# Attention: pieces of other work in halves, between the two pairs of scores of a step

## The chip, the cores and the metric

The kernel runs on one core of one Trainium2 chip. The metric is the device time of one execution in microseconds (us). Before the change the median of three runs is 5130.76 us (5127.3 to 5130.8).

## The reference

A sequence of 4096 rows of width 256 goes through four stages, each added to its input: attention, expert layer, attention, expert layer.

```
x = x + attention_a(layernorm(x))
x = x + experts(layernorm(x))
x = x + attention_b(layernorm(x))
x = x + experts(layernorm(x))
```

Both attentions have 16 heads of width 16 and a causal mask. Attention a also adds exp(denom_bias) to each row's sum of exponentials and has a bias behind its output weights. Per head:

```
sim   = q @ k.T / 4, masked above the diagonal
e     = exp(sim - max(sim))
out   = (e @ v) / (sum(e) [+ exp(denom_bias)])
y     = concat(out over heads) @ Wo.T [+ bo]
```

The expert layer computes logits of 4096 rows against 2048 slots (64 experts of 32), two softmaxes of them (over slots and over experts), the slots' inputs, a small matrix product per expert, and the weighted sum back to the rows.

## The kernel before

All matrix work is float32. The rows stay in SBUF as `x`, 32 tiles of 128 rows. An attention takes the rows in 8 blocks of 512 and the heads in 4 groups of 4; a unit is one group in one block of queries, and the units run block after block, 32 in all. Keys and queries are split into a high and a low part (`split`, L165), so that two passes of reduced precision add up to float32; the parts are written to DRAM (`kd`, `qd`) and read back in the layout that the scores need (`load_to`, L345).

A unit needs two passes. Pass A (`steps_a`, L367) computes scores with queries on the partitions and takes each row's maximum on VectorE (L388 for blocks on the diagonal, with the mask added, L394 for the others). `finish_a` negates the maxima and sends them through DRAM into a layout in which a matmul can add them. Pass B (`steps_b`, L446) computes the scores transposed, keys on the partitions. One of its steps handles 128 keys: two pairs of heads, and for each pair two matmuls of keys and queries (`sc<-q,k`), two that subtract the maxima (`sc<-qm,one`), and one exponential on ScalarE (L471). On the diagonal GpSimd sets what lies above it to zero (L475), and the scores are narrower by `off` columns. `weigh` (V in what follows, L426) multiplies the exponentials of a step by the values, one step later. Every unit ends with `epilogue`: the sums go through DRAM to be inverted (`invert`), the output is divided on GpSimd (`divide`), and after four groups it is fetched again (`fetch`) and projected (`project`, L530).

TensorE's order is the program's. The loop at L601 writes it by hand: a step's two pairs of scores, half of the pass A work that is due (`wanted` spreads pass A of later units over the steps), a piece of other work (`net.beside`), V of the step before, the rest of pass A. Pass A, the pieces and the projections take their PSUM banks in turn from one pool of three (`net.bank`); the scores of pass B have two buffers of two banks, V one bank. Instructions of other engines are placed by the framework's scheduler, unless the code pins them.

`net.beside(n)` (L79) advances a clock by n, calls what is due (`invert`, `divide`, `fetch`), and then takes one piece, from `urgent` (projections) or from `side`. The side pieces of a block (`pieces`, L186) prepare the keys, queries and values of the block four ahead: four normalizations on GpSimd, two turns (four transposes each), four of keys and queries (512 columns each, `part`), two of values (`dense_values`), with empty places between. Blocks 0 and 1 of the second attention are prepared in the last loop of the first expert stage, one piece per tile from tile 7 on; what is left then runs after that loop, with one PSUM bank. Blocks 2 and 3 (and 0 and 1 of the first attention) are made all at once ahead of the steps, by `dense`.

Of the kernel before, what the change touches and what calls it, by code (L numbers as in the profile page):

```python
# [19 lines left out]
P = 128  # L20
S = 4096
D = 256
NT = S // P
QB = 512
NQB = S // QB
H = 16
HD = 16
# [15 lines left out]
class _Net:  # L43
# [22 lines left out]
    def mm(self, *a, **k):  # L66
        self.tc.keep_in_program_order(self.nc.tensor.matmul(*a, **k))  # L67
# [38 lines left out]
class _Attention:  # L106
# [55 lines left out]
            nc.gpsimd.tensor_tensor(x[:, t, :], x[:, t, :], self.bot, ALU.add)  # L162
        return y

    def split(self, ps, cc, dst, key, part=None):  # L165
        nc = self.net.nc
        two = part is not None
        if not two:
            part = self.hl[self.nhl % 2]
            self.nhl += 1  # L170
        hi, lo = part[:, 0, :], part[:, 1, :]
        nc.scalar.copy(hi.bitcast(F32R), ps)
        nc.vector.tensor_tensor(lo.bitcast(F32R), ps, hi, ALU.subtract)
        if key:
            nc.sync.dma_start(
                dst[ts(cc, 8)].bitcast(F32).rearrange("h e r l t -> (h e) r (l t)"),
                part.rearrange("p l t -> p (l t)").unsqueeze(1).to_broadcast([P, 2, 2 * QB]),
            )
            return
        for r in range(2):  # L180
            (nc.scalar if two and r else nc.sync).dma_start(
                dst[ts(cc, 8), :, :, r].bitcast(F32).rearrange("h e l t -> (h e) l t"), part
            )


    def pieces(self, b, fast=False, values=True):  # L186
        net, nc = self.net, self.net.nc
        xb, ys = self.xb[b % 2], {}
        idle = lambda: None

        def scale(i):
            if i == 0:
                self.begin(b)
            ys[i] = self.norm(4 * b + i, fast)

        def turn(t2):
            ps = net.bank().rearrange("p (c i t) -> p c i t", c=2, i=2)
            for i in range(2):
                for c in range(2):
                    net.tr(ps[:, c, i, :], ys[2 * t2 + i][:, ts(c, P)])  # L200
            nc.scalar.copy(xb[:, :, ts(t2, 2 * P)], ps.rearrange("p c i t -> p c (i t)"))

        def part(w, cc, key):
            ps = net.bank()
            for c in range(2):
                net.mm(ps, w[:, c, ts(cc, P)], xb[:, c, :], start=c == 0, stop=c == 1)
            self.split(ps, cc, (self.kd if key else self.qd)[b], key)

        out = []
        for t2 in range(2):  # L210
            out += [lambda i=i: scale(i) for i in (2 * t2, 2 * t2 + 1)]
            out += [idle, lambda t2=t2: turn(t2), idle]
        for w, key in ((self.wk, True), (self.wq, False)):
            out += [lambda a=(w, cc, key): part(*a) for cc in range(2)]
        if values:
            out += self.dense_values(b)
        return out

    def values(self, b, t2, ps):
        net, xb = self.net, self.xb[b % 2]  # L220
        ps = ps.rearrange("p (i d) -> p i d", i=2)
        for i in range(2):
            for c in range(2):
                net.mm(
                    ps[:, i, :], xb[:, c, ts(2 * t2 + i, P)], self.wv[:, c, :],
                    start=c == 0, stop=c == 1,
                )
        net.nc.scalar.copy(
            self.vah[:, ds(4 * b + 2 * t2, 2), :, 0:HD],
            ps.rearrange("p i (h e) -> p i h e", e=HD),  # L230
        )
# [32 lines left out]
    def run(self, ready, experts):  # L264

        net, tc, nc = self.net, self.net.tc, self.net.nc
        x, mm = net.x, net.mm
        bo, db = self.bo, self.db
        self.xd = net.xd = net.xds.pop(0)
        with ExitStack() as ctx:  # L270
            pool = lambda n, b, **k: ctx.enter_context(tc.tile_pool(name=f"at_{n}", bufs=b, **k))
            cp = pool("c", 1)
            wo = self.wo
# [10 lines left out]
                out=maskw, in_=maskw, compare_op=ALU.is_ge, fill=NEG,  # L284
# [11 lines left out]
            for p in range(2):  # L296
                f = net.ep.tile([P, QB], F32, name="ot", bufs=3)[:, 0:P]
                nc.gpsimd.memset(f, 0.0)
                for h2 in range(2):
                    for l in range(2):  # L300
                        nc.gpsimd.affine_select(
                            out=f, in_=f, compare_op=ALU.not_equal, fill=1.0,
# [30 lines left out]
            def third():  # L333
                actx.close()
                pairs.extend([psb, pool("psc", 1, space=PSUM)])
                net.banks = pool("psx", 1, space=PSUM)
# [148 lines left out]
            def epilogue(u, ot):  # L485
                g, b = units[u]
                if g == 0:
                    self.ad[b] = net.dram.tile([2 * P, QB], F32, name=f"{self.name}o{b}")
                d16 = net.ep.tile([P, 16], F32, name="d16", bufs=3)
                dd = net.dram.tile([P, 16], F32, name="dd", bufs=3)  # L490
                nc.sync.dma_start(d16, ot[HD:P:32, :].rearrange("j (c s) -> j c s", s=16))
                rb = {}

                def invert():
                    if db is not None:
                        nc.vector.tensor_scalar(d16, d16, edb[:, g : g + 1], None, ALU.add)
                    nc.vector.reciprocal(d16, d16)
                    rb[0] = net.ep.tile([P, QB], F32, name="rb")
                    nc.sync.dma_start(dd, d16)
                    nc.sync.dma_start(  # L500
                        rb[0],
                        dd.rearrange("(j c) s -> j (c s)", j=HG).unsqueeze(1)
                        .to_broadcast([HG, 32, QB]),
                    )
                    net.after(8, divide)

                def divide():
                    on = rb[0]
                    nc.gpsimd.tensor_tensor(on, ot, on, ALU.mult)
                    for j in range(HG):  # L510
                        nc.sync.dma_start(
                            self.ad[b][ds((HG * g + j) * HD, HD), :], on[ds(32 * j, HD), :]
                        )
                    if g == NG - 1:
                        net.after(4, fetch)

                back = {}

                def fetch():
                    for i2 in range(2):  # L520
                        ao = net.ep.tile([P, 2, 2 * P], F32, name="ao", bufs=2)
                        nc.sync.dma_start(
                            ao, self.ad[b].rearrange("(c p) t -> p c t", p=P)[:, :, ts(i2, 2 * P)]
                        )
                        back[i2] = ao
                    net.after(
                        8, lambda: net.urgent.extend([lambda: project(0), lambda: project(1)])
                    )

                def project(i2):  # L530
                    ps = net.bank().rearrange("p (i d) -> p i d", i=2)
                    for i in range(2):
                        for c in range(2):
                            mm(
                                ps[:, i, :], back[i2][:, c, ts(i, P)], wo[:, c, :],
                                start=c == 0, stop=c == 1,
                            )
                    xs = x[:, ds(4 * b + 2 * i2, 2), :]
                    nc.vector.tensor_tensor(xs, ps, xs, ALU.add)
                    if i2:  # L540
                        nc.sync.dma_start(self.xd[:, ts(b, 4), :], x[:, ts(b, 4), :])

                net.after(6, invert)
# [11 lines left out]
            def maxima_to(n):  # L555
                while done_a[0] < min(n, total):
                    next(runs)
                    done_a[0] += 1
# [31 lines left out]
            n = 0  # L590
            for u, (g, b) in enumerate(units):
                if g == 0 and 4 <= b + 4 < NQB:
                    net.side.extend(self.pieces(b + 4))
                if g == 0 and b == NQB - 1:
                    experts.load()

                last = deque()
                if u == len(units) - 1:
                    last.extend(experts.ahead())
                    third()  # L600
                for p, _ in enumerate(steps_b(u)):  # L601
                    n += 1
                    if last and p % 4 == 3 and p >= 8 * (b + 1) - 4 * len(last):
                        last.popleft()()
                    if p % 2 == 0:
                        continue
                    while (
                        g >= 2 and net.side and u + 2 < len(units)
                        and units[u + 2][1] > max(3, b)
                    ):  # L610
                        net.beside()
                    want = wanted(n + 1)
                    maxima_to((done_a[0] + want) // 2)
                    net.beside(2)
                    values_to(1)
                    maxima_to(want)
            values_to(0)
# [621 lines left out]
```

## Time and profile before

| | us |
|---|---|
| median of three runs | 5130.76 |
| the profiled execution | 5132.21 |
| its span | 5130.5 |
| TensorE (PE) busy | 4975.7 |
| VectorE (DVE) busy | 4154.9 |
| ScalarE (ACT) busy | 2631.2 |
| GpSimd (POOL) busy | 1155.7 |
| maxima of pass A, L394, 3584 of 681 ns | 2222.8 |
| all passes of 512 columns, `bank<-zone`, 256 of them | 131.7 |
| first attention's exponentials, from and to | 87 to 1784 |
| second attention's exponentials, from and to | 2653 to 4347 |

The mean granted clock of TensorE was 0.989 of full speed. One float32 matmul shows as two instructions where the operands aren't split. Ends of matmuls are modelled in the profile: two that follow each other closely overlap in the rows, so the distance from start to start tells what one costs. PEld is TensorE's loading of weights. In a timeline the columns are start, duration, engine, line, operation, output and inputs, shape, how many were merged, and, in brackets, the engine's idle time before it and what ended it.

### The profile page before, as it was taken

What the parts mean: (1) busy time and instruction counts of PE and PEld (TensorE: products, weight loads), DVE (VectorE), ACT (ScalarE), POOL (GpSimd) and SP (SyncE); (2) the same over time, 40 slices, a digit from 0 to 9 for tenths busy, and PEclk for the clock granted to TensorE, in tenths of its full rate; (3) what the DMA queues carried; (4) which work ended last, traced back from release to release, by engine and by line L of the source; (5) the groups of instructions that cost most, each with busy time, mean ns of one, the idle gap of its engine ahead of it and who ended that gap; (6) DMA issues with size and microseconds to landing.
All of it is one profiled execution on the core that took longest, in us unless ns stands there. A gap on an engine that the chain in (4) does not pass through costs nothing.

```text
span 5130.5 us, 79443 instructions
## 1 busy us (share of the span) xinstructions
PE 4975.7 (97%) x29936; PEld 2672.1 (52%) x29936; DVE 4154.9 (81%) x7800; ACT 2631.2 (51%) x3112; POOL 1155.7 (23%) x1088
## 2 busy tenths in 40 slices
PE   7999999999999999999989999999999999999999
PEld 4444454445445444458854444545444454444588
DVE  5678989898989378887757789898989893888876
ACT  3466666667666721223225666666676667212222
POOL 3211000000000155554411110000000001555554
PEclk9999999999999999999999999999999999999999
DMA  7433222222211023443454332222211110234443
GB/s 255 144 109 125 66 77 65 65 61 66 61 62 57 24 80 114 140 148 120 145 181 145 108 126 69 73 65 65 65 62 61 62 57 23 83 112 149 141 146 110
DMA packets 266449, 499.17 MB, mean 97 GB/s; under 512 B 44976, under 2 KB 110000, under 8 KB 258384
## 3 DMA queue, kind: packets, MB, share of 16 engines
q1 hardware_dynamic: 260832, 485.57, 28.8%
q10 hardware_dynamic: 4896, 7.87, 0.5%
q8 instruction: 235, 3.85, 0.3%
q14 instruction: 150, 1.23, 0.1%
q0 software_dynamic: 336, 0.66, 0.0%
HBM read 336.73 MB, written 156.76 MB: 96 GB/s over the span
## 4 chain that ended last, share of the span: by engine, by line
PE 82%; DVE 11%; DMA 3%; ACT 2%; issue 2%; POOL 1%; SPq 0%; DVEq 0%; ACTq 0%; POOLq 0%
PE o L67 26%; PE bank L67 21%; PE sc L67 17%; PE acc L67 8%; PE lg L67 8%; DVE mx L394 5%; DVE junk L388 3%; PE ps L70 2%; ACT pb L471 1%; DMA rb<-dd 1%; PE bank L70 0%; DMA d<-ot 0%; DVE lT L949 0%; DVE st L94 0%; DMA l<-ld 0%
## 5 line engine op out<-in xcount | busy, mean ns | idle before, releaser
L471 ACT ACTIVATE pb<-sc 128x1024 f32<-128x1024 f32 (+3 forms) x2304 | 2070.4, 951 | 1126.8 <-PE sc L67 1125.4
L394 DVE TENSOR_REDUCE mx<-bank 128x1 f32<-128x512 f32 x3584 | 2222.8, 681 | 153.9 <-PE bank L67 148.0
L67 PE MATMUL bank<-k,q 64*128 64x512 f32 (+3 forms) x4608 | 1332.9, 451 | 64.5 <-DVE mx L394 26.7
L67 PEld LDWEIGHTS bank<-k,q 64*128 64x128 f32 x4608 | 663.8, 185 | 1175.9 <-DVE mx L394 768.4
L67 PE MATMUL o<-pb,va 128*32 128x512 f32 (+3 forms) x9216 | 1158.1, 573 | 4.2 <-POOL pb L475 2.5
L67 PE MATMUL sc<-q,k 64*128 64x512 f32 (+3 forms) x4608 | 982.0, 389 | 11.8 <-ACT pb L471 11.5
L67 PE MATMUL sc<-qm,one 64*128 64x512 f32 (+3 forms) x4608 | 944.8, 377 | 0.0
L388 DVE CUSTOM_DVE_ANT_0 junk<-bank,maskw 128x128 bf16<-128x128 f32 (+3 forms) x1024 | 502.4, 491 | 255.3 <-PE bank L67 147.2
L475 POOL TENSOR_SCALAR_AFFINE_SELECT pb<-pb 128x256 f32<-128x256 f32 x512 | 205.0, 407 | 2167.3 <-ACT pb L471 2160.8
L67 PEld LDWEIGHTS sc<-q,k 64*128 64x128 f32 x4608 | 506.9, 187 | 130.5 <-issue 50.6
L67 PEld LDWEIGHTS sc<-qm,one 64*128 64x128 f32 x4608 | 523.1, 187 | 69.2
L67 PE MATMUL acc<-e,x 128*128 128x512 f32 x1008 | 460.4, 600 | 8.6 <-POOL e L700 8.5
L693 ACT ACTIVATE e<-e 128x1024 f32<-128x1024 f32 x126 | 133.3, 1058 | 650.8 <-POOL e L692 650.8
L67 PE MATMUL o<-ys,lT 128*128 128x256 f32 x2048 | 457.8, 380 | 0.0
L67 PE MATMUL lg<-zone,xnT 128*128 128x512 f32 x1008 | 453.1, 592 | 1.2 <-ACT xnT L972 1.2
L67 PEld LDWEIGHTS o<-ys,lT 128*128 128x128 f32 x2048 | 384.5, 191 | 56.0 <-issue 6.6
L67 PEld LDWEIGHTS o<-pb,va 128*32 128x32 f32 x9216 | 183.5, 108 | 314.1 <-issue 284.8
L891 POOL TENSOR_TENSOR e<-l,mc 128x1024 f32<-128x1024 f32 x120 | 281.3, 2366 | 280.4 <-DMA l<-ld 190.5
L692 POOL TENSOR_TENSOR e<-l,m 128x1024 f32<-128x1024 f32 x126 | 240.9, 1912 | 422.7 <-DVE m L691 418.3
L67 PEld LDWEIGHTS acc<-e,x 128*128 128x128 f32 x1008 | 190.0, 192 | 244.5 <-issue 229.0
L67 PEld LDWEIGHTS lg<-zone,xnT 128*128 128x128 f32 x1008 | 190.3, 190 | 234.3 <-issue 223.4
L677 DVE TENSOR_TENSOR l<-lg,zone 128x512 f32<-128x512 f32 x252 | 172.5, 688 | 134.0 <-PE lg L67 128.2
(136 smaller groups left out, 3216.6 us busy)
## 6 DMA issues: line engine op xcount, KB each, us to landing
k<-ak SPq DMA_DIRECT2D x144, 512.0 KB
k<-bk SPq DMA_DIRECT2D x144, 512.0 KB
ld<-l SPq DMA_DIRECT2D x126, 512.0 KB
l<-ld SPq DMA_DIRECT2D x60, 1024.0 KB
w<-in_L_ffn_expert_w_dram SPq DMA_DIRECT2D x26, 1024.0 KB
q<-aq SPq DMA_DIRECT2D x32, 512.0 KB
rb<-dd SPq DMA_DIRECT2D x64, 256.0 KB
q<-bq SPq DMA_DIRECT2D x32, 512.0 KB
```

The source lines that it names most:

```text
L67: self.tc.keep_in_program_order(self.nc.tensor.matmul(*a, **k))
L70: self.tc.keep_in_program_order(self.nc.tensor.transpose(o, i, self.ident))
L388: nc.vector.tensor_tensor_reduce(out=junk[:, 0:w], in0=scs[h2][:, 0:w], in1=maskw[:, QB - w : QB], scale=1.0, scalar=-3e38, op0=ALU.add, o ...
L394: nc.vector.tensor_reduce(m, scs[h2], AX.X, ALU.max)
L471: nc.scalar.activation(pb[:, :, off:QB], sc[:, :, off:QB], AF.Exp)
L475: nc.gpsimd.affine_select(out=d, in_=d, compare_op=ALU.is_ge, fill=0.0, base=0, pattern=[[0, 2], [1, P]], channel_multiplier=-1,)
L677: pin(net.nc.vector.tensor_tensor(l, lg, self.phb[:, ds(h * (E // 2) + n * 512, 512)], ALU.add))
L692: pin(nc.gpsimd.tensor_tensor(e3, l3, _bc(m.unsqueeze(2), [P, ne, SLOT]), ALU.subtract))
L693: nc.scalar.activation(e, e, AF.Exp)
L891: pin(nc.gpsimd.tensor_tensor(e[:, ns, :], l, _bc(cms[t].unsqueeze(1), [P, NH, SLOT]), ALU.subtract))
```

## The change

Every piece for keys and queries becomes two of 256 columns (`part` with `n`); a half has its own copy on ScalarE and subtraction on VectorE, and the transfer to DRAM follows the second half. Value pieces are one tile of 128 rows each (`value`) in place of two; projections likewise, four `project(i)` in place of two. The call of `net.beside(2)` moves from behind the first half of pass A to the place behind a step's first pair of scores.

```diff
-    def split(self, ps, cc, dst, key, part=None):
+    def split(self, ps, cc, dst, key, part=None, n=None):
         nc = self.net.nc
         two = part is not None
         if not two:
+            self.nhl += n == 0
             part = self.hl[self.nhl % 2]
-            self.nhl += 1
-        hi, lo = part[:, 0, :], part[:, 1, :]
+        cut = part if n is None else part[:, :, ts(n, QB // 2)]
+        hi, lo = cut[:, 0, :], cut[:, 1, :]
         nc.scalar.copy(hi.bitcast(F32R), ps)
         nc.vector.tensor_tensor(lo.bitcast(F32R), ps, hi, ALU.subtract)
+        if n == 0:
+            return
         if key:
...
-        def part(w, cc, key):
-            ps = net.bank()
+        def part(w, cc, key, n):
+            ps = net.bank()[:, 0 : QB // 2]
             for c in range(2):
-                net.mm(ps, w[:, c, ts(cc, P)], xb[:, c, :], start=c == 0, stop=c == 1)
-            self.split(ps, cc, (self.kd if key else self.qd)[b], key)
+                net.mm(
+                    ps, w[:, c, ts(cc, P)], xb[:, c, ts(n, QB // 2)],
+                    start=c == 0, stop=c == 1,
+                )
+            self.split(ps, cc, (self.kd if key else self.qd)[b], key, n=n)
...
         for w, key in ((self.wk, True), (self.wq, False)):
-            out += [lambda a=(w, cc, key): part(*a) for cc in range(2)]
+            out += [lambda a=(w, cc, key, n): part(*a) for cc in range(2) for n in range(2)]
         if values:
-            out += self.dense_values(b)
+            out += [lambda t=t: self.value(b, t) for t in range(4)]
         return out
+
+    def value(self, b, t):
+        net, xb = self.net, self.xb[b % 2]
+        ps = net.bank()[:, 0:D]
+        for c in range(2):
+            net.mm(ps, xb[:, c, ts(t, P)], self.wv[:, c, :], start=c == 0, stop=c == 1)
+        net.nc.scalar.copy(
+            self.vah[:, 4 * b + t, :, 0:HD], ps.rearrange("p (h e) -> p h e", e=HD)
+        )
...
-                        8, lambda: net.urgent.extend([lambda: project(0), lambda: project(1)])
+                        8, lambda: net.urgent.extend([lambda i=i: project(i) for i in range(4)])
...
-                def project(i2):
-                    ps = net.bank().rearrange("p (i d) -> p i d", i=2)
-                    for i in range(2):
-                        for c in range(2):
-                            mm(
-                                ps[:, i, :], back[i2][:, c, ts(i, P)], wo[:, c, :],
-                                start=c == 0, stop=c == 1,
-                            )
-                    xs = x[:, ds(4 * b + 2 * i2, 2), :]
+                def project(i):
+                    ps = net.bank()[:, 0:D]
+                    for c in range(2):
+                        mm(
+                            ps, back[i // 2][:, c, ts(i % 2, P)], wo[:, c, :],
+                            start=c == 0, stop=c == 1,
+                        )
+                    xs = x[:, 4 * b + i, :]
                     nc.vector.tensor_tensor(xs, ps, xs, ALU.add)
-                    if i2:
+                    if i == 3:
                         nc.sync.dma_start(self.xd[:, ts(b, 4), :], x[:, ts(b, 4), :])
...
                     if p % 2 == 0:
+                        net.beside(2)
                         continue
...
                     want = wanted(n + 1)
                     maxima_to((done_a[0] + want) // 2)
-                    net.beside(2)
                     values_to(1)
                     maxima_to(want)
```

## The prediction

> **What bounds the kernel now.** I read the page first (busy shares, chain), then the groups of instructions, then TensorE's timeline in single steps of the attention, where all of the change but one place lies. In the page:
>
> ```profile
> PE 4975.7 (97%) x29936; PEld 2672.1 (52%) x29936; DVE 4154.9 (81%) x7800; ACT 2631.2 (51%) x3112; POOL 1155.7 (23%) x1088
> PE 82%; DVE 11%; DMA 3%; ACT 2%; issue 2%; POOL 1%; SPq 0%; DVEq 0%; ACTq 0%; POOLq 0%
> L394 DVE TENSOR_REDUCE mx<-bank 128x1 f32<-128x512 f32 x3584 | 2222.8, 681 | 153.9 <-PE bank L67 148.0
> L67 PEld LDWEIGHTS bank<-k,q 64*128 64x128 f32 x4608 | 663.8, 185 | 1175.9 <-DVE mx L394 768.4
> ```
>
> PE heads the chain, but its weight loads for the maxima's scores stood 768 us behind VectorE's maxima: PE's 97% hides short waits for a free bank. Which engine ends a step has to be read from the steps. TensorE's timeline of one plain step (block 3, no piece, full widths):
>
> ```profile
> 508.40 0.50 PE L67 MATMUL bank<-k,q 64*128 64x512 f32 x2
> 508.74 0.40 PE L67 MATMUL sc<-q,k 64*128 64x512 f32 x2
> ...
> 509.44 0.40 PE L67 MATMUL sc<-qm,one 64*128 64x512 f32 x2
> 509.67 0.52 PE L67 MATMUL bank<-k,q 64*128 64x512 f32 x2
> 510.11 1.06 PE L67 MATMUL o<-pb,va 128*32 128x512 f32 x8
> 511.11 0.50 PE L67 MATMUL bank<-k,q 64*128 64x512 f32 x2
> ```
>
> The step is 511.11 - 508.40 = 2.71 us. PE's own work is about 2.6. VectorE shows four maxima in 2.48 and 0.22 idle. Such a step is just PE-bound. A step against the diagonal is not: scores and V are narrower (by the same starts PE needs about 2.40, 1.95, 1.66 us at offsets 128, 256, 384, and 1.96 in the next unit's first), but the four maxima stay, and the four steps take 2.51, 2.42, 2.75, 2.39. Steps with masked 512-wide maxima (0.84 us each) take 3.2. There VectorE is the bound.
>
> **What a piece costs today.** A step of block 3 with a 512-column key piece:
>
> ```profile
> 473.83 0.52 PE L67 MATMUL bank<-k,q 64*128 64x512 f32 x2
> 474.44 1.98 PE L67 MATMUL bank<-zone 128*128 128x512 f32 x4
> 476.36 1.06 PE L67 MATMUL o<-pb,va 128*32 128x512 f32 x8
> 477.35 0.50 PE L67 MATMUL bank<-k,q 64*128 64x512 f32 x2
> ```
>
> The last maxima before began at 472.57; 477.35 - 472.57 = 4.78 us against 2.71: the piece adds 2.07, 1.92 of it its own (476.36 - 474.44), 0.1 a wait for a bank. Nothing is hidden, even where VectorE is the bound (4.51 and 4.68 at offsets 256 and 384): the piece is queued behind the maxima's banks, and then VectorE runs dry. Projections add 2.1, value pieces 2.0.
>
> **Part 1: halves between the pairs of scores.** Per attention 16 key and query pieces, 8 of values and 14 of projection (seven blocks; the eighth's fall in the stage after) become 76 halves. Eight 256-column passes elsewhere take 1.92 too (2602.45 to 2604.37 us), so a pass is (1.92 - 0.2)/8 = 0.215 and a half's four passes 0.86. Columns cost nothing extra; place does. The scores run in two halves of 64 rows, a piece on all 128 rows. PE going from scores to V and back, in the last unit, which has no maxima:
>
> ```profile
> 1731.95 0.40 PE L67 MATMUL sc<-q,k 64*128 64x512 f32 x2
> 1732.19 0.39 PE L67 MATMUL sc<-qm,one 64*128 64x512 f32 x2
> 1732.51 1.07 PE L67 MATMUL o<-pb,va 128*32 128x512 f32 x8
> 1733.50 0.50 PE L67 MATMUL sc<-q,k 64*128 64x512 f32 x2
> ```
>
> Scores follow scores after 0.23, V follows after 0.32: +0.09. V's 8 end 0.99 after they began, 0.1 more than two rounds of 0.445. The first pair after V needs 0.34 (1731.38 to 1731.72) instead of 0.23: +0.11. A piece's own first weights show another 0.1. Ahead of V the piece stood at a change that PE made anyway; between two pairs of scores it makes one of its own: 0.86 + 0.09 + 0.1 + 0.1 + 0.11 = 1.26 us. Here rules of the skill bear on the row. The Trainium skill, "TensorE: Matmul & The Clock Gate", section "Step-by-step: what each phase is for", has weights for the background buffer pulled ahead of running matmuls: by that a half costs 0.86, two of them 1.72, and 38 x 2 x (2.05 - 1.72) = 25 us go. The page "TensorEngine Tiling (Array Packing)", section "Key Properties", says that a change of tiling mode drains the engine, which speaks against the change. The row sides with the second, with about 0.1 us a side; two halves then cost PE 2.52 where one piece cost 1.92. I take 1.26; ends 0.86 and, with a further 0.2 of unseen bank or weight wait, 1.45.
>
> Against this stands cover. By the new order a half takes its bank from the maxima of a step earlier, long read, and VectorE works off the former step's last two maxima meanwhile. In the full-width step: scores to +0.8 us after the former maxima's start, half to 1.95, second pair to 2.5, maxima, V, end 3.86; ScalarE copies the half out between its two exponentials (0.38), VectorE subtracts by 2.65 and has the next maximum at 2.9. So +1.15 a step. At an offset of 384 VectorE's 4 x 0.60 + 0.36 nearly equals PE's 1.66 + 1.26: +0.25. Against masked 512 steps +0.6, in steps with six maxima +0.1 to 0.3.
>
> Summed over the stretches that hold the halves (start to start of exponentials; PE's sum plus 1.26 a half, or VectorE's where longer):
> - block 7's pieces and the projection of block 2, 16 steps: before 463.81 to 522.23 = 58.4; after 38.5 + 16 x 1.26 = 58.7. Nothing.
> - block 6, with a table change of ScalarE that stalls it 2 us: before 60.7 (63.0 in the second attention); after 36.3 + 20.2 + 2 = 58.5. -3.
> - block 5, with many six-maxima steps: before 194.64 to 279.90 = 85.3; after 79 + 1.5 (table change) + 0.9 (a denominator's landing) = 81. -4.5 with its turn.
> - block 4: before 53.1, where PE's own sum is only 38, so that the rest is VectorE's waits for landings; after 40.7 + waits. -1 (between +4 and -6).
> - projections of blocks 3 to 6, full width: 4 x (4 x 1.15 - 2 x 2.1) = +1.6 to 2.
> - eight turns (four 128-column transposes each): two changes of mode more, partly covered: +1.
>
> Together -5 per attention, -10 for both.
>
> **Part 2: the pieces beside the first expert stage.** Its loop has 25 places (tiles 7 to 31), one piece each. Before, 28 pieces: three run after the loop. After, 36: eleven do, a turn and eight halves among them. There each waits for the one bank:
>
> ```profile
> 2591.35 1.88 PE L67 MATMUL bank<-zone 128*128 128x512 f32 x4
> 2593.27 0.58 ACT L172 CAST zone<-bank 128x512 fp32r<-128x512 f32 x1 [0.26 <-PE bank L67]
> 2593.88 0.69 DVE L173 TENSOR_TENSOR zone<-bank,zone 128x512 fp32r<-128x512 f32 x1 [0.33 <-DMA bk<-zone]
> 2594.63 1.98 PE L67 MATMUL bank<-zone 128*128 128x512 f32 x4 [1.40 <-DVE zone L173]
> ```
>
> Three rounds of 3.4 took 8.9 us to the last pass. A half's round is 0.96 + 0.38 + 0.42 + 0.2 = 1.95; the tail becomes 1.35 (turn) + 7 x 1.95 + 0.96 = 16.0. The loop sheds 2.2 of PE work. Net +4.9. Nothing covers it: what follows needs PE.
>
> **Part 3: what moves with it.** The delayed steps (reciprocal of denominators, division, fetch) are now issued ahead of the second pair too. In the compiled order the reciprocals keep their place among the maxima but for eleven of 64, moved by one to four, mostly earlier. A reciprocal that is early holds VectorE, and behind it the maxima and PE's banks; one such wait was 2.1 us. I take +2 (-2 to +8). SyncE's transfers are as many as before: kd and qd still leave once per two halves. GpSimd's division lies one exponential earlier, in front of the second diagonal mask; V needs that only a step later. Copies add about 0.17 us to ScalarE and 0.1 to VectorE a pair, covered above.
>
> **Sum.** Against the profiled execution (5132.2; span 5130.5): -10 + 5 + 2 = -3. The median of the runs is 1.5 lower, 5130.8, so 5128.
>
> **Rivals.**
> 1. Wash (the forecast): 5128, own range 5120.5 to 5141. 0.36.
> 2. Cover wins: mode changes overlap with waits, a half costs about 1.05, and half of block 4's 15 idle us come back: 152 x 0.2 x 0.6 = -18 and 2 x -5 more: 5100 (5085 to 5120). For it: before's piece steps beat PE's own sums by 7 to 15 us a stretch. Against: the full-width steps show PE with no slack. 0.33.
> 3. Cover fails, TensorE's changes of mode stay bare: every half adds 1.26 over a full-width step, so 76 x (2 x 1.26 - 2.05) = +36, +5 for the tail: up to 5172, 5152 if half the cover is lost. It decides once a half adds over 1.0 us on average (78 us of pieces per attention / 76, less the tail). Place: between the pairs of scores. 0.31.
> 4. VectorE held by early reciprocals: +10 to 15 on the forecast, 5140; inside 3's share.
>
> **Numbers.** Differences within 0.2% (10 us) are about what a measurement of this kernel can't tell from none. Faster 0.33, same 0.36, slower 0.31. The range leaves out a tenth on either side: 5095 to 5155.
>
> **What would show it.** Right: a half's step in block 3 at full width of 3.8 to 3.9 us, diagonal steps with halves at 2.9 to 3.3, PE's waits behind the maxima gone from these steps; first-to-second-score gaps with a half of 1.4 to 1.5 us; the seam after the first expert stage 5 us longer; block 5's stretch about 81. Wrong: full-width steps at 3.5 (rival 2) or over 4 (rival 3), or another wait of VectorE ahead of a subtraction, since the copy out stands behind the first exponential.

## The result and the profile after

The changed kernel takes 5146.66 us (median of 7 runs, 5141.33 to 5152.24) against 5130.53 (7 runs of the kernel before, 5127.3 to 5133.79): ratio 1.0028, interval 1.0019 to 1.0037. It is slower by 0.28%, 16 us. The forecast was 5128, with slower as the least likely of the three outcomes. The profiled execution took 5144.56 us, its span is 5142.8, its mean clock 0.989, as before.

The page of the changed kernel, with the rows that answer to those shown of before (busy time of the engines; the chain that ended last; the maxima; the weight loads for the maxima's scores):

```profile
PE 4992.3 (97%) x30096; PEld 2677.4 (52%) x30096; DVE 4177.5 (81%) x7872; ACT 2654.4 (52%) x3168; POOL 1156.0 (22%) x1088
PE 85%; DVE 9%; ACT 2%; issue 1%; DMA 1%; POOL 1%; DVEq 0%; SPq 0%; ACTq 0%; POOLq 0%
L410 DVE TENSOR_REDUCE mx<-bank 128x1 f32<-128x512 f32 x3584 | 2226.7, 682 | 153.7 <-PE bank L67 144.4
L67 PEld LDWEIGHTS bank<-k,q 64*128 64x128 f32 x4608 | 644.9, 185 | 1147.9 <-DVE mx L410 758.5
```

VectorE's share of the chain fell from 11 to 9%, TensorE's rose from 82 to 85%. The weight loads still stand 758.5 us behind the maxima (768.4 before), VectorE's maxima still stand 144.4 us behind TensorE (148.0), and TensorE is busy 17 us longer.

The stages tell where the 12.3 us between the two spans lie. An attention is counted from its first exponential to its last, the loop of the first expert stage from there to its last weighing matmul, the seam from there to the second attention's first scores. All in us, from the timelines of one profiled execution each; the last four columns answer to experiments below. The four stages of after sum to 15.3 more; 1.8 less from the seam's end to the second attention's first exponential and 1.2 less outside all of these, which was not followed, make up the difference.

| | before | after | halves ahead of V | whole, between the pairs | two banks in the seam | no pieces left for the seam |
|---|---|---|---|---|---|---|
| first attention | 1696.6 | 1699.7 | 1699.4 | 1705.6 | 1701.3 | 1702.7 |
| expert loop | 807.9 | 807.6 | 806.9 | 809.7 | 809.9 | 823.0 |
| seam | 10.2 | 25.8 | 22.6 | 10.2 | 18.0 | 6.2 |
| second attention | 1693.8 | 1690.5 | 1698.3 | 1700.3 | 1693.2 | 1694.4 |
| span | 5130.5 | 5142.8 | 5147.7 | 5145.6 | 5143.6 | 5150.2 |

The seam took 15.6 us more, not 7. The attentions together took nothing less, where 10 were to be won. One profile is not enough to tell a few us. Three profiles with the order of before give means of 1697.5 and 1690.5 for the attentions, five with the order of after 1701.4 and 1693.5. The first attention of before spreads from 1696.4 to 1699.4, the second from 1685.4 to 1693.8: the 4 us more of the first stand just clear of that, the 3 of the second don't. The seam of after has a spread too: three more profiles with the same code there (halves ahead of V, and the longer and the shorter halves below) show 22.5 to 22.6 us, 12.3 to 12.4 more than before.

**The full-width step is what the prediction said.** TensorE's timeline of the changed kernel, block 3, a step with a half (start, duration, engine, line, operation):

```profile
502.28 0.50 PE L67 MATMUL bank<-k,q 64*128 64x512 f32 x2
502.62 0.39 PE L67 MATMUL sc<-q,k 64*128 64x512 f32 x2
502.85 0.40 PE L67 MATMUL sc<-qm,one 64*128 64x512 f32 x2
503.18 1.13 PE L67 MATMUL bank<-zone 128*128 128x256 f32 x4
504.24 0.50 PE L67 MATMUL sc<-q,k 64*128 64x512 f32 x2
...
505.13 1.07 PE L67 MATMUL o<-pb,va 128*32 128x512 f32 x8
506.12 0.50 PE L67 MATMUL bank<-k,q 64*128 64x512 f32 x2
```

From 502.28 to 506.12 is 3.84 us; 3.8 to 3.9 was predicted. The second pair comes 1.39 after `sc<-qm,one` where it would come 0.23 after without a half: 1.16 for the half, of which 0.86 are its passes. TensorE shows no wait in this step.

**A step with six maxima is not.** All engines of the changed kernel in block 1, around the start of a step at 234.09 us:

```profile
230.97 3.92 DVE L410 TENSOR_REDUCE mx<-bank 128x1 f32<-128x512 f32 x6
233.15 0.49 PE L67 MATMUL bank<-k,q 64*128 64x512 f32 x1 [0.34 <-DVE mx L410]
233.15 0.44 PE L67 MATMUL sc<-q,k 64*128 64x384 f32 x1
233.92 1.13 PE L67 MATMUL bank<-zone 128*128 128x256 f32 x4
235.44 0.39 PE L67 MATMUL bank<-k,q 64*128 64x512 f32 x2
235.50 0.42 DVE L174 TENSOR_TENSOR zone<-bank,zone 128x256 fp32r<-128x256 f32 x1 [0.61 <-ACT zone L173]
235.86 1.29 DVE L410 TENSOR_REDUCE mx<-bank 128x1 f32<-128x512 f32 x2
```

TensorE works in the order of the program. It is held at the last scores for the maxima until a bank is free (233.15), then does a pair of scores, the half and the second pair, and only then has new scores for the maxima ready (235.44 and after). At 233.15 VectorE had 1.74 us of work left; the stretch takes 2.3. So VectorE runs dry at 234.89, waits 0.61 for the half's copy (ScalarE, L173) and then does the half's own subtraction. The cover was there, but too short.

**The seam runs at half the clock.** The changed kernel behind the expert loop:

```profile
2595.03 1.13 PE L67 MATMUL bank<-zone 128*128 128x256 f32 x4 [0.68 <-ACT zone L204]
2597.38 1.13 PE L67 MATMUL bank<-zone 128*128 128x256 f32 x4 [1.22 <-DVE zone L174]
2599.45 2.08 PE L67 MATMUL bank<-zone 128*128 128x256 f32 x4 [0.95 <-DVE zone L174]
2602.45 2.07 PE L67 MATMUL bank<-zone 128*128 128x256 f32 x4 [0.92 <-DVE zone L174]
2604.56 0.37 ACT L173 CAST zone<-bank 128x256 fp32r<-128x256 f32 x1 [2.62 <-PE bank L67]
2604.97 0.43 DVE L174 TENSOR_TENSOR zone<-bank,zone 128x256 fp32r<-128x256 f32 x1 [2.57 <-ACT zone L173]
2605.45 2.08 PE L67 MATMUL bank<-zone 128*128 128x256 f32 x4 [0.92 <-DVE zone L174]
```

The first two halves take 1.13 us each, from the third on 2.08, the same four passes. The stretches of the seam (busy time of PE, PEld, DVE, ACT, POOL; then the granted clock, the DMA share, GB/s), first before, then after, then halves ahead of V, whose seam is the same code:

```profile
2591.30:2600.00 8.70, 5.85 (x14) 2.26 (x14) 2.90 (x7) 2.47 (x5) 4.76 (x10) 1.00 1.00 361
```

```profile
2594.00:2599.40 5.40, 2.61 (x12) 1.47 (x10) 2.28 (x7) 3.79 (x7) 4.77 (x10) 0.97 0.84 269
2599.40:2614.40 15.00, 10.37 (x20) 5.88 (x20) 2.10 (x5) 1.86 (x5) 0.00 (x0) 0.50 0.73 263
```

```profile
2592.30:2604.20 11.90, 6.25 (x26) 3.74 (x25) 3.60 (x10) 4.91 (x10) 4.77 (x10) 1.00 0.80 299
2604.20:2614.40 10.20, 8.36 (x18) 5.65 (x19) 1.27 (x3) 1.12 (x3) 0.00 (x0) 0.50 0.85 279
```

In the first stretch of after TensorE is busy 2.61 us of 5.40, since each half waits for the one bank; then the granted clock is 0.50 for fifteen microseconds and more. In halves ahead of V the same rounds kept 1.00 for 11.9 us, and the clock fell only then; the longer and the shorter halves show 11.9 and 11.6. That it falls is common to all four profiles, after how long is not. Before, three pieces of 512 columns with waits of 1.4 us between them kept 1.00. The Trainium skill, "TensorE: Matmul & The Clock Gate", section "A second HAM failure mode: psum-queue depth-cycling", tells of the same: brief idling of TensorE between groups, as it cycles through banks, and a clock that falls to half. Its section "HAM oscillation — how this bites in real kernels" gives as the rule that no idle gap may exceed about 3.4 us; here no gap between two halves was over 1.22, and the clock fell, so keeping to the rule was not enough. By the durations that the prediction took from a full clock a round is 1.95 us; measured it is 2.05 to 2.10 at the full clock (after a first one of 2.34) and 3.00 at half.

### The profile page after: what moved, and what is told of

Its sections match the earlier page's. It is cut to its first block, busy times and chain, and to the rows that moved or that the text cites. A ratio compares the mean times of both kernels' runs of the same rounds, so it can differ in the third digit from the quotient of the medians.

```text
span 5142.8 us, 79915 instructions
## 1 busy us (share of the span) xinstructions
PE 4992.3 (97%) x30096; PEld 2677.4 (52%) x30096; DVE 4177.5 (81%) x7872; ACT 2654.4 (52%) x3168; POOL 1156.0 (22%) x1088
## 4 chain that ended last, share of the span: by engine, by line
PE 85%; DVE 9%; ACT 2%; issue 1%; DMA 1%; POOL 1%; DVEq 0%; SPq 0%; ACTq 0%; POOLq 0%
PE o L67 26%; PE bank L67 21%; PE sc L67 18%; PE acc L67 8%; PE lg L67 8%; DVE mx L410 4%; DVE junk L404 3%; PE ps L70 2%; ACT pb L487 1%; PE bank L70 0%; DMA d<-ot 0%; DVE lT L964 0%; POOL e L906 0%; DVE nr L425 0%; DVE x L981 0%
## 5 line engine op out<-in xcount | busy, mean ns | idle before, releaser
L410 DVE TENSOR_REDUCE mx<-bank 128x1 f32<-128x512 f32 x3584 | 2226.7, 682 | 153.7 <-PE bank L67 144.4
L67 PE MATMUL bank<-k,q 64*128 64x512 f32 (+3 forms) x4608 | 1301.2, 448 | 61.6 <-DVE mx L410 29.7
L67 PEld LDWEIGHTS bank<-k,q 64*128 64x128 f32 x4608 | 644.9, 185 | 1147.9 <-DVE mx L410 758.5
L67 PE MATMUL sc<-q,k 64*128 64x512 f32 (+3 forms) x4608 | 1003.4, 395 | 11.1 <-ACT pb L487 10.8
```

The costliest lines, as they stand in the source:

```text
L410: nc.vector.tensor_reduce(m, scs[h2], AX.X, ALU.max)
```

## The experiments

Each experiment is set against runs of the kernel before on the same chip: 5133.61 us (22 runs) for the first four, 5131.92 (25) for the next four, 5131.88 (21) for the last three. Single runs of it spread by up to 7 us to either side, so stages of the profiles are read beside the medians.

**Which part costs: halves alone, the move alone.** The first experiment has the halves, but the call stays ahead of V; the second moves the call and leaves pieces and projections whole.

```diff
 # e1_halves_alone, against after
                     if p % 2 == 0:
-                        net.beside(2)
                         continue
...
                     maxima_to((done_a[0] + want) // 2)
+                    net.beside(2)
                     values_to(1)
 # e2_move_alone, against before: the same lines the other way round
```

> Halves as in the changed kernel, but the call for a piece stays behind the first maxima, ahead of V. If the place costs (a half between two pairs of scores makes TensorE change its array's mode for itself): full-width steps with a half fall from 3.84 to about 3.65 us, and the whole to about 5138, since the tail after the first expert stage stays as long as in the changed kernel (+13 us against before). If the place pays (bank waits gone), steps rise above 3.84 and the whole to 5155.

> Whole pieces as before, taken between the two pairs of scores. The stage of the experts is then as before. If the growth of the changed kernel lies in that stage alone: 5131, within 5 us of before. If the place itself costs: each of the 38 pieces of an attention adds 2.12 instead of 2.05 and keeps VectorE waiting longer, 5140 or more.

Halves alone took 5155.14 us, ratio 1.0036 (1.0024 to 1.0049); the move alone 5142.43, ratio 1.0015 (1.0006 to 1.0024). Both cost. Halves bring the long seam (22.6 us) at either place. The move of whole pieces leaves the seam at 10.2 and adds 9 and 7 us to the attentions: 38 pieces each, so some 0.2 us a piece. For halves the place makes no clear difference (1699.4 and 1698.3 ahead of V, means of 1701.4 and 1693.5 between the pairs).

A change of TensorE between 64 and 128 rows on the piece's own account does not by itself explain the 0.2, since halves lose nothing by the place. Full-width steps with projections, from exponential to exponential, take 2.71 us without a piece; with a half they take 3.93 ahead of V and 3.86 between the pairs, where 3.65 ahead of V would have shown that the place costs: for a half it pays a little, the second expectation. With a whole piece they take 4.82 and 5.11. Two projections, first halves ahead of V, then whole between the pairs:

```profile
1178.70 1.13 PE L67 MATMUL bank<-zone,ao 128*128 128x256 f32 x4
1182.63 1.13 PE L67 MATMUL bank<-zone,ao 128*128 128x256 f32 x4
```

```profile
1177.84 0.69 DVE L539 TENSOR_TENSOR x<-bank,x 128x512 f32<-128x512 f32 x1 [1.17 <-PE bank L67]
1179.96 0.18 PEld L67 LDWEIGHTS bank<-k,q 64*128 64x128 f32 x1 [0.23 <-DVE mx L394]
```

In the second, VectorE stands idle for 1.17 us until the piece is there (0.83 to 0.96 in the same step of before), and its next maxima come only behind that; then TensorE's next scores for the maxima wait 0.23 for a bank. That is lost cover again, read from one step and not tested by itself.

**Is it the seam?** The changed kernel with whole pieces beside the expert stage only:

```diff
-            out += [lambda a=(w, cc, key, n): part(*a) for cc in range(2) for n in range(2)]
+            out += [lambda a=(w, cc, key, n): part(*a) for cc in range(2)
+                    for n in ((0, 1) if values else (None,))]
```

> The changed kernel, but the key and query pieces that run beside the first expert stage stay whole (28 pieces, three after the loop, as before). If the eleven pieces after the loop are the loss: 13 us less than the changed kernel, 5133, with the second attention's first exponential at 2656 in place of 2669. If the loss is in the attentions: no more than 5 us less, 5141.

5137.49 us, ratio 1.0008 (0.9999 to 1.0017), midway between the two expectations. The seam is 10.2 again, the span 5.7 us shorter than after's. The medians say that 9 or 10 of the 16 us lie in the seam; what is left, some 4 to 6, points to the attentions.

**Is it the clock?** Eight transposes of no use behind each piece of the seam keep TensorE busy while it waits for the bank:

```diff
             while net.side:
                 net.beside(3)
+                fill = pools["t"].tile([P, 512], F32, name="ps")
+                for i in range(8):
+                    tr(fill[:, ts(i % 4, P)], net.ident)
```

> The changed kernel, with eight transposes of the identity into an unused bank behind each piece of the tail, work that no result uses. If the tail's rounds of 3.0 us come from TensorE's clock, which stood at 0.50 there while TensorE was idle half the time: the clock stays at 1.0, rounds fall to 2.0 to 2.2 although TensorE has more to do, and the whole falls by 6 to 8 to 5139. If the rounds are long for another reason (the queue of transfers, banks): rounds of 3.0 or longer, 5147 or more.

The seam of that kernel, TensorE and ScalarE, and its clock:

```profile
2601.64 1.13 PE L67 MATMUL bank<-zone 128*128 128x256 f32 x4
2602.61 1.04 PE L70 MATMUL ps<-ident 128*128 128x128 f32 x8
2603.69 1.13 PE L67 MATMUL bank<-zone 128*128 128x256 f32 x4
2608.20 0.37 ACT L173 CAST zone<-bank 128x256 fp32r<-128x256 f32 x1 [2.97 <-DMA bk<-zone]
2609.09 1.13 PE L67 MATMUL bank<-zone 128*128 128x256 f32 x4 [1.34 <-DVE zone L174]
```

```profile
2597.60:2609.00 11.40, 9.96 (x62) 8.00 (x60) 2.09 (x5) 2.25 (x6) 2.60 (x7) 1.00 0.95 363
2609.00:2616.80 7.80, 7.62 (x44) 6.25 (x44) 1.31 (x4) 1.12 (x3) 0.00 (x0) 1.00 0.90 287
```

With TensorE busy the clock stays at 1.00 to the end and a round is 2.05 us, 0.95 less than at half the clock: that the idling brought the clock down is shown. The seam is 22.1 us, 3.7 shorter than in the profile of after but hardly shorter than the 22.5 of the other three, since the transposes take about 2 us ahead of the first half, and one half waits 3.34 from start to start for its buffer, which SyncE is still writing out (`bk<-zone`). The median, 5149.0 (ratio 1.0029, 1.0017 to 1.0041), shows no gain: the filling keeps the clock, but it wins no time.

**Two banks in the seam.**

```diff
+            bank, net.bank = net.bank, lambda: banks[len(net.side) % 2]()
+            banks = (bank, banks[1])
             while net.side:
                 net.beside(3)
+            net.bank = bank
```

> The changed kernel with two banks in place of one for the eleven pieces behind the first expert stage's loop. If the seam is long because each half waits for the one bank, and the granted clock falls because TensorE idles meanwhile, then rounds fall from 2.1 to 3.0 us to about 1.2, the clock stays at 1.0, the seam falls from 25.8 to 12 to 15 us, the time to about 5135. If the halves wait for the buffers that SyncE still writes out, the seam stays above 20 us and the time above 5142.

5142.37 us, ratio 1.0016 (1.0007 to 1.0025), the seam 18.0. The changed kernel with two banks:

```profile
2604.20 2.00 PE L67 MATMUL bank<-zone 128*128 128x256 f32 x8 [0.56 <-DVE zone L174]
2607.88 0.65 ACT L173 CAST zone<-bank 128x256 fp32r<-128x256 f32 x2 [3.83 <-DMA bk<-zone]
2608.76 2.58 PE L67 MATMUL bank<-zone 128*128 128x256 f32 x8 [2.56 <-DVE zone L174]
2612.51 3.78 PE L67 MATMUL bank<-zone 128*128 128x256 f32 x8 [1.16 <-DVE zone L174]
```

Two halves now go back to back in 2.0 us (8 passes), until the two buffers are full: ScalarE's copy waits 3.83 us for a transfer, TensorE idles 2.56, and the clock falls after all, so that the last eight passes take 3.78. Both expectations were half right. The bank is the first limit, the buffers that are written out the second, and here too the clock fell behind a long idle stretch.

**Could the loop take them?** A second piece in a tile of the expert loop whenever more pieces than tiles are left, in the changed kernel (e5) and in the one before (e6):

```diff
                     weigh(t, half, NEC)
+                    if beside and len(net.side) > NT - 1 - t:
+                        net.beside(3)
```

> The changed kernel, but the loop of the first expert stage takes a second piece in a tile as long as more pieces are left than tiles, so that none is left behind the loop. If the seam of 25.8 us comes from nothing but the pieces standing alone there (one bank, TensorE idle half the time), the seam falls to under 4 us and the loop pays for eleven pieces' TensorE work only, some 11 us: 5146 - 22 + 11 = about 5135. If a piece costs as much in the loop, because it waits for its one bank there too, nothing is won: 5143 or more.

> The kernel before with the same loop: its last three pieces are taken inside the loop. The seam of 10.2 us falls to under 4 us, the loop pays three passes of 2 us: 5131 - 7 + 6 = about 5130, no difference. If the loop hides TensorE's passes (its tiles are not TensorE-bound throughout), 5124.

The changed kernel took 5148.66, ratio 1.0031 (1.0021 to 1.0041), the one before 5135.53, ratio 1.0006 (0.9997 to 1.0015). The seams fell to 6.2 and 7.0 us, the loops grew by 15.4 and 6.9. In the loop a half costs 1.08 us and a whole piece 1.93, start to start of the weighing matmuls around it, which is TensorE's time for it: nothing covers it there either. So the three pieces of before cost 5.8 of the 6.9, and the seam gave only 3.2, since TensorE now stands idle 4.51 us ahead of the first scores, while SyncE is still fetching their keys and queries. In the changed kernel eight halves account for 9 of the 15 us; one wait in the tile of a turn makes 5 more, and 32 weighing matmuls behind it take 9.48 in place of 7.07, at a mean clock of 0.74 (TensorE):

```profile
2482.11 7.07 PE L67 MATMUL o<-ys,lT 128*128 128x256 f32 x32
...
2496.10 1.12 PE L70 MATMUL ps<-ident,e 128*128 128x128 f32 x4 [5.06 <-DVE lT L964]
2497.01 9.48 PE L67 MATMUL o<-ys,lT 128*128 128x256 f32 x32
```

**How bare is a half?** One more contraction in every half of the attentions, then one less. The longer one does the first contraction twice, the second time over the first; the shorter one leaves out the second half of every sum of keys, queries, values and projections.

```diff
 # e7_longer_halves: in part, and alike in value and project
-            for c in range(2):
+            for i, c in enumerate((0, 0, 1) if values else (0, 1)):
 ...
-                    start=c == 0, stop=c == 1,
+                    start=c == 0 , stop=c == 1 or (values and i == 0),
 # e9_shorter_halves: in part, and alike in value and project
+            last = 0 if values else 1
-            for c in range(2):
+            for c in range(last + 1):
```

> The changed kernel with a third contraction in every half of the attention stages (the first one is done twice, the second time over the first): 0.43 us more of TensorE per half, nothing else. Where TensorE sets the step it comes out in full, where VectorE's maxima set it and the half is covered it does not show. By the cover that the prediction assumed, the stretches of blocks 0 and 1 and the diagonal and masked steps of blocks 2 and 3 take less than half of it: blocks 0 to 1 of the first attention (some 28 halves) grow by under 6 us, block 2 and block 3 (16 each) by under 5. If the half is bare everywhere, since TensorE's order puts it between scores that VectorE is waiting for, they grow by about 12, 7 and 7. Blocks 4 to 7 (16 projections in full-width steps) grow by 7 in either case.

> The changed kernel with one contraction in place of two in every half of the attention stages (the second half of each sum of keys, queries, values and projections is left out): 0.43 us less of TensorE per half, the same order, the same changes of mode, the same copies. The longer halves took 60 us more of 65 added. If TensorE ends every step that has a half already at two contractions, the time falls by as much: 152 x 0.43 = 65 to about 5082. If the cover that the prediction counted on exists, but is smaller than a half (VectorE's four maxima end the diagonal and the masked steps once a half is short), then the first two blocks fall by less than 6 us of 12 and the whole by 35 to 50, to about 5100 or more, while the 16 projections in full-width steps fall by 7.

The longer halves took 5211.47 us, ratio 1.0153 (1.0134 to 1.0171): 65 more than after. The groups of the pieces' matmuls by shape (busy, mean ns), after and longer halves:

```profile
L67 PE MATMUL bank<-zone 128*128 128x256 f32 x576 | 166.5, 420 | 18.2 <-DVE mx L404 9.5 <-DVE zone L174 6.8 <-ACT va L244 1.2
L67 PE MATMUL bank<-zone,ao 128*128 128x256 f32 x256 | 71.5, 402 | 0.0
```

```profile
L67 PE MATMUL bank<-zone 128*128 128x256 f32 x768 | 204.7, 405 | 12.7 <-DVE zone L174 6.8 <-DVE mx L407 4.1 <-ACT va L247 1.2
L67 PE MATMUL bank<-zone,ao 128*128 128x256 f32 x384 | 99.2, 395 | 0.0
```

TensorE got 38.2 + 27.7 = 65.9 us more to do, and the time grew by 65: taken together it is bare. By stages of single profiles (against the mean of the five with the same order) the attentions grew by 26 and 34 us of 33 each. Blocks 0 and 1 alone grew by 7 and 9 of 12, which lies between the two expectations.

The shorter halves took 5106.17, ratio 0.9950 (0.9932 to 0.9968): 40 less, not 65. Read by the total alone, this is the second expectation, a cover that ends the step once the half is short. Read by the step, it is not. Steps of block 1 in the first attention, us:

| maxima, offset | before, no piece | shorter | after | longer |
|---|---|---|---|---|
| six, 0 | 3.96 | 4.64 | 5.01 | 5.44 |
| six, 128 | 3.77 | 4.37 | 4.78 | 5.20 |
| six, 256 | 3.62 | 4.22 | 4.44 | 4.87 |
| six, 384 | 3.89 | 5.75 | 4.73 | 5.18 |
| six, 0 (next unit) | 3.45 | 6.25 | 4.76 | 5.20 |
| four, 0 | 3.15 | 3.30 | 3.73 | 4.17 |
| four, 128 | 2.50 | 3.17 | 3.50 | 3.94 |
| four, 256 | 2.42 | 3.02 | 3.16 | 3.59 |
| four, 384 | 2.76 | 3.18 | 3.44 | 3.90 |

Longer halves add 0.42 to 0.46 us in every one of them. Shorter ones take 0.33 to 0.43 away at offsets 0 and 128, and 0.14 to 0.26 where the diagonal leaves TensorE least to do (256 and 384): only there is another engine close behind. And two steps became longer by 1.0 and 1.5 us with less to do. Their windows, the shorter halves first (columns as above), then after:

```profile
239.30:243.52 4.22, 3.92 (x25) 1.90 (x26) 4.04 (x8) 1.54 (x3) 0.81 (x2) 1.00 0.24 94
243.52:249.27 5.75, 5.39 (x25) 2.39 (x25) 5.07 (x9) 1.14 (x3) 0.81 (x2) 0.63 0.64 233
249.27:255.52 6.25, 6.01 (x25) 3.08 (x26) 3.81 (x12) 2.95 (x4) 0.00 (x0) 0.50 0.38 123
```

```profile
238.87:243.31 4.44, 4.24 (x27) 2.23 (x28) 3.93 (x8) 1.56 (x3) 0.81 (x2) 1.00 0.20 77
243.31:248.04 4.73, 4.53 (x27) 2.27 (x28) 4.30 (x8) 1.14 (x3) 0.81 (x2) 1.00 0.50 164
248.04:252.81 4.77, 4.39 (x27) 2.28 (x28) 3.85 (x10) 2.88 (x5) 0.00 (x0) 1.00 0.82 282
```

The clock was granted at 0.63 and 0.50 there. The same holds of the stages. Against the mean of the five profiles with the same order, blocks 0 and 1 together fell by only 1 and 2.5 us of 12 in the two attentions, at mean clocks of 0.66 to 0.72 and 0.92 to 0.93, where the five have 0.74 to 0.82 and 0.96 to 0.99. Blocks 2 and 3, at 1.00, fell by 13 and 9 of 14, blocks 4 to 7 by 5 and 5 of 7. So most of what is missing is missing where the clock was lower; how much of it the clock took was not separated.

**A version from the parts that help.** Blocks 4 to 7 hold only projections and took 1 to 3 us less with halves, in either place. And the seam of before, with its three whole pieces, is short enough for a second bank to help.

```diff
 # e10_before_two_banks: before, with the diff of e8
 # e11_before_two_banks_projections: also
-                        8, lambda: net.urgent.extend([lambda: project(0), lambda: project(1)])
+                        8, lambda: net.urgent.extend([lambda i=i: project(i) for i in range(4)])
 # and project(i) as in the changed kernel; net.beside stays ahead of V
```

> The kernel before with two banks in place of one for the three pieces behind the first expert stage's loop: the attentions as before, the seam from 10.2 to about 7 us, since the pass need not wait for the copies of the piece ahead: 5131 - 3 = 5128, at the edge of what can be told. If the buffers that SyncE writes out set it: no change, 5131.

> The kernel before with two banks in that seam and with the projections alone in halves of 256 columns, at their old place ahead of V. Blocks 4 to 7 took 1.8 and 2.5 us less with halves ahead of V, so this gives -3 for the seam and -4 for the attentions: 5124. If a half costs more than half a piece here too (56 halves at 0.2 more), 5131 + 8 = 5139.

With two banks alone 5128.41, ratio 0.9994 (0.9984 to 1.0003), the seam 6.8 as expected, within what can be told from nothing. With the projections in halves as well 5122.72, ratio 0.9983 (0.9974 to 0.9992): faster than both kernels. Blocks 4 to 7 took 1147.2 and 1146.4 us (before 1149.6 and 1150.7). The one profile, taken of the slowest of the 11 runs, has a seam of 6.8, but its attentions as wholes, 1696.3 and 1694.1, are no shorter than before, as blocks 0 and 1 of the second took 6 more. So the 9 us of the median are measured, but only in part placed.

## Why the prediction was wrong

Two steps failed: the cover of Part 1, by most, and the length of a round in Part 2. By its own steps:

- **A half in a full-width step, 3.8 to 3.9 us: right** (3.84), with the changes of mode at 0.1 us a side that it read from the row (1.16 for the half where it took 1.26). The weights pulled ahead, which would have made it 3.5, did not show. What it said of the place did not hold: ahead of V a full-width step with a half is not shorter (3.93).
- **The stretches of Part 1: the sum failed**, and with it the 10 us of gain; by the means the attentions took 4 and 3 us more. In us, first and second attention:

| stretch | before | predicted | after |
|---|---|---|---|
| block 4's pieces, first 26 steps | 107.6, 101.5 | 1 less | 105.5, 102.0 |
| block 5's, 22 steps | 85.3, 85.2 | 81 | 87.9, 86.5 |
| block 6's, 16 steps | 60.7, 63.1 | 58.5 | 61.0, 59.3 |
| block 7's, 16 steps | 58.4, 58.4 | 58.7 | 60.9, 60.6 |
| blocks 4 to 7 | 1149.6, 1150.7 | 1.6 to 2 more | 1148.6, 1147.3 |

  (Of block 6's 63.1 in before, 1.7 lie in one step at a clock of 0.72, so the change won about 2 there, not 4.) The failed step is the cover in "steps with six maxima +0.1 to 0.3" and "at an offset of 384 +0.25". Seven steps with six maxima took 0.82 to 1.31 us more than the same steps without a piece, 6.9 together where the prediction has 1.4: that is most of the miss in block 5. At an offset of 384 it was 0.68 with four maxima and 0.84 with six. The diagonal steps with four maxima took 3.16 to 3.50 with a half at offsets of 128 to 384, where 2.9 to 3.3 was predicted. The prediction compared sums of each engine's work in a step and took the longer; the order of TensorE's queue, in which the half stands between VectorE's last scores and its next, was left out. Over the whole attention the third contraction, nearly all of it bare, shows the same. What the doubled copies and subtractions add by themselves was not tested.
- **The table change of ScalarE, 2 us: about right.** It now falls on a block's fourth projection: that step takes 6.15 us in block 3, its neighbours with a half 3.8, so it costs 2.3 there.
- **Part 2, the pieces behind the expert loop: the size failed.** The mechanism was right (eleven pieces, each behind the one bank): predicted 7.1 more for the seam and 2.2 less for the loop, measured 12.3 to 15.6 more and 0.3 less. The mis-sized term is the round of 1.95 us. In the profile of after five of the seven took 2.99 to 3.04, at a granted clock of 0.50, one 2.07 and one 2.35, and the two value pieces that follow ran at half the clock as well. Where the clock fell later (halves ahead of V) there was a first round of 2.34 and four of 2.05 to 2.10. With such rounds to the end the seam would be about 19.5 us (an estimate from that profile and from before's last passes): some 2 us of the miss are the rounds themselves, 3 to 6 the clock. All durations in that term were read where the clock was full, and it was not asked whether TensorE would be busy enough in the new seam to keep it. In the loop the halves gave back 1.65 of the 2.2 (3 turns and 8 halves at 0.65 and 1.08, for 4 turns and 5 pieces at 0.65 and 1.93); profiles of the same loop differ by 3 us, so the rest can't be told.
- **Part 3, reciprocals: within its range.** Their waits for landed sums are 29.5 us after and 30.4 before, within the -2 to +8 that was left open; the +2 was not needed.
- **Rivals.** "Cover fails" named the mechanism and its threshold: it decides "once a half adds over 1.0 us on average". By its own accounting (78 us of pieces an attention, and 3 to 4 more measured, over 76 halves) a half adds 1.07. Its time, 5152 with half of the cover lost, was 5 us over the 5146.66, with a seam that supplied most of the loss in place of the attentions. "Cover wins" falls. Block 0's units took 4 and 7 us less, but only 25 of the 48 passes of block 4's halves still ran there, the rest in block 1, whose units took 5 and 9 more.

What stays open in part: why the projections in halves come out 1 to 3 us shorter in blocks 4 to 7, where two halves of 1.15 should cost more than one piece of 2.1. Some of it lies in the step of the table change. Before, that step has no piece and takes 4.86 us, 2.15 more than a plain one. With the fourth half in it, it takes 5.67 between the pairs and 5.21 ahead of V (4.86 in block 5), where the two costs added up would be 6.0 and 6.1: a part of the half is hidden in the table change there.

## What to carry to other kernels

Cover for a moved piece of work has to be read in the order of the queue that issues it, not from sums of two engines: ask how much work the other engine still holds at the moment the piece starts, and whether it outlasts the piece and what stands behind it. To split a piece doubles its fixed part (copies, waits for a bank): look for the place where the pieces run alone. And a duration read at a full clock holds only where TensorE stays busy enough to keep that clock: look at the clock's column before you reuse it.

## What the runs showed of the hardware

- Rounds of about 1.1 us of TensorE's work in 2.05 to 2.35 brought the granted clock down to 0.50 in all four profiles that have them, 5 us behind the expert loop in one and 12 in three, with no idle time above 1.22 us between two halves; rounds of 2.05 filled with useless transposes kept it at 1.00. Three rounds with 1.9 us of work in 3.4 kept it too; they were over after 9 us.
- An idle stretch of 5.06 us inside the expert loop was followed by 9.3 us at a mean clock of 0.74.
- Two steps with less work for TensorE were longer, at a lower clock: in one of them 25 instructions in 6.25 us at a clock of 0.50, against 27 in 4.77 at 1.00. TensorE shows 6.01 us busy in that step, so its busy share doesn't warn; the clock's column does.
